# Where VectorE adds the bias to the messages, and where it makes the last block's sums, in a two-layer graph network

## The chip, the cores and the metric

The kernel runs on one core of a Trainium2 chip. The metric is the device time of one execution in microseconds (us); the kernel before takes 2246.47 us, the median of three runs (2245.61 to 2249.44). Inside a run the clock is not constant: some runs have stretches of 3.4 us at half of it (0.50).

Names used below: TensorE does matrix products and writes them into PSUM, which has eight banks here; VectorE, ScalarE and GpSimd do the elementwise work. In the profile they are PE, DVE, ACT and POOL. L386 is line 386 of the kernel.

## The reference, cut to what matters

64 graphs of 256 nodes with 256 features pass through two layers in fp32. Layer 0 has a conv branch and a message branch that meet in GRU gates; layer 1 is a graph convolution.

```python
h = relu(bn1(conv1d(xc, conv1_w, 0)))                  # xc is x with nodes and features swapped
x_conv = relu(bn2(conv1d(h, conv2_w, 8)) + xc)         # 17 taps
s = x @ w_se.T + b_se
A = exp(-dist(s)) * adj
msg = relu(x @ w_msg.T + b_msg)
x_nmp = einsum('bnm,bmd->bnd', A, msg)
gi = concat(x_conv, x_nmp) @ w_ih.T + b_ih
gh = x @ w_hh.T + b_hh                                 # r and z from gi + gh
nn_ = tanh(gi_n + r * gh_n)
x = layernorm(x + (1 - z) * nn_ + z * x)
# layer 1
h = layernorm(x)
conv = (adj @ h) @ W_rel + b_rel + h @ W_root
x = layernorm(x + x + relu(conv))
```

## The kernel before

The 64 graphs go in eight batch blocks of eight. While the gates and messages of block b run graph by graph, the conv branch of block b+1 is fed in between them: `pump()` takes the next pieces of the conv generator, butterflies of a transform on VectorE (L104, L362) and products on TensorE (L386). The order of the Python calls is the order of each engine's instructions.

The messages of graph k+3 are made while graph k passes. Two halves of the nodes go into two PSUM banks; VectorE then adds the biases, two small and two 256-wide additions. Only then are the banks free.

```python
def bank(name):
    return psum.tile([P, 512], F32, tag="ps", name=name)      # eight banks, handed out in turn

def messages(k, idle=False):
    ...
    pss = [bank("ps_msg") for _ in range(C)]
    for m, ps in enumerate(pss):
        for c in range(C):
            nc.tensor.matmul(ps[:, :D + 4], XT[k][:, c, m * P:(m + 1) * P], wms[:, c, :], ...)   # L678
    yield                                                     # <- step(msg) resumes here
    for m, ps in enumerate(pss):
        ...
        nc.vector.tensor_add(twice[:, m, :, 0:3], ...)                                           # L688
        nc.vector.tensor_add(MSG[k][:, m, :], ps[:, :D], bms[:, :D])                             # L690
    nc.scalar.activation(MSG[k], MSG[k], AF.Relu)
    ...                                                       # five small steps on GpSimd, L696 to L700

def products(b, first, sums):
    p1, p2, p3 = bank("ps_k1"), bank("ps_k2"), bank("ps_k3")  # the next three banks
    ...                                                       # 24 matmul records, L386
    def take():
        nc.scalar.copy(k1, p1)                                # L404
        ...                                                   # VectorE takes p3 and p2, L405, L406
```

The main loop, up to the last conv block, and the loop of the last batch block, which has no conv work left:

```python
for k in range(b * BG, min((b + 1) * BG, B - 1)):             # blocks 0 to 6
    ...
    msg = messages(k + 3) if k + 3 < B else None
    step(msg)                     # the eight matmuls of the messages
    step(up)                      # nn: two VectorE operations, tanh on ScalarE
    pump()                        # a piece of the next block's conv
    step(msg)                     # the four additions
    step(up)                      # w, L877, and its statistics
    pump()
    step(up)                      # h, L896
    ...

for k in range(first_k, B - 1):                               # block 7
    load(k + 3)
    load_x(k + 1)
    ga, up = block_gates(k), update(k)
    step(ga)                      # first half of the gates: seven-product form, from sums of blocks
    step(y_left)                  # output of the graph before: add, statistics (VectorE)
    step(ga)
    transposes_h(k - 1)
    step(ga)
    passing(k + 1)
    if k + 2 < B:
        factors(k + 2)
    step(ga)                      # x's part of n: eight matmuls and the addition L858
    if k + 2 < B:
        block_sums(k + 1, 0)      # four 128-wide additions each, L808 to L811
        block_sums(k + 1, 2)
    project(k - 1)
    ...
    msg = messages(k + 3) if k + 3 < B else None
    step(msg)
    step(up)
    step(msg)
    step(up)
    if k + 2 < B:
        block_sums(k + 1, 1)
    ...
```

`block_gates` takes the products of the gates (L826) out of PSUM with VectorE additions at L831.

```python
def pump():
    ...                           # conv pieces up to the share due at this point
    if STAGE.get(NB - 1) in ("inverse", "out"):
        next(sums_left, None)     # one pair of additions for the weights of the last block
    if STAGE.get(NB - 1) == "out" and (NB - 1) * BG in NMP and len(early_sums) > (done < 1e8):
        block_sums((NB - 1) * BG, early_sums.pop(0))
```

Of the kernel before, what the change touches and what calls it, by code (L numbers as in the profile page):

```python
# [17 lines left out]
B, N, D = 64, 256, 256  # L18
# [58 lines left out]
def gnn_two_layers(  # L77
# [22 lines left out]
    def bank(name):  # L100
        return psum.tile([P, 512], F32, tag="ps", name=name)
# [548 lines left out]
    def load(k):  # L650

        if k >= B:
            return
        load_xt(k)
        load_adj(k)
# [9 lines left out]
    def load_x(k):  # L665
        if k < B:
            XG[k] = work.tile([P, C, D], F32, tag="x", name="x")
            nc.sync.dma_start(out=XG[k], in_=x[k].rearrange("(c p) d -> p c d", p=P))
# [59 lines left out]
    def mask(k):  # L728
        nc.vector.tensor_mul(AT[k], AT[k], ADJ[k])
# [15 lines left out]
    def gates_rz(k, n):  # L745
        if n == 0:
            RZ[k] = (work.tile([P, C, 2 * D], F32, tag="rz", name="rz", bufs=1),
                     work.tile([P, C, 2 * D], F32, tag="gn", name="gn", bufs=1))
        q, ins = inputs(k, n)
        prz = bank("ps_rz")  # L750
        for c in range(C):
            nc.tensor.matmul(prz, XT[k][:, c, q], whh[:, c, 0:2 * D], start=(c == 0), stop=False)  # L752

        for j, i in enumerate((2, 3, 0, 1) if k == 0 else range(4)):
            nc.tensor.matmul(prz, ins[i], wih[:, i, 0:2 * D], start=False, stop=(j == 3))  # L755
        rz = RZ[k][0]

        nc.vector.tensor_add(rz[:, n, :], prz, brzn[:, :2 * D])  # L758
        nc.scalar.activation(rz[:, n, :], rz[:, n, :], AF.Tanh, scale=0.5)  # L759

    def gates_n(k, n):
        q, ins = inputs(k, n)
        pn = bank("ps_n")
        for c in range(C):
            nc.tensor.matmul(pn[:, D:], XT[k][:, c, q], whh[:, c, 2 * D:], start=(c == 0), stop=(c == C - 1))  # L765
        for i, t in enumerate(ins):
            nc.tensor.matmul(pn[:, :D], t, wih[:, i, 2 * D:], start=(i == 0), stop=(i == 3))  # L767
        nc.vector.tensor_add(RZ[k][1][:, n, :], pn, brzn[:, 2 * D:])  # L768
# [29 lines left out]
    def block_sums(k, i):  # L798

        if i == 2:  # L800
            xc, g = XC[k]
            v = xc[:, :, g, :]
        else:
            v = (XT, NMP)[i][k]
        a11, a12, a21, a22 = (v[:, c, n * P:(n + 1) * P] for n in range(C) for c in range(C))
        at = S * D + ((k % 2) * 3 + i) * 4 * P
        s1, s2, s3, s4 = (XF[:, at + j * P:at + (j + 1) * P] for j in range(4))
        nc.vector.tensor_add(s1, a21, a22)  # L808
        nc.vector.tensor_sub(s2, s1, a11)
        nc.vector.tensor_sub(s3, a11, a21)  # L810
        nc.vector.tensor_sub(s4, a12, s2)  # L811
        LEFT[k, i] = (a11, a12, s4, a22, s1, s2, s3)
# [54 lines left out]
    def update(k):  # L867

        rz, gn = RZ[k]
        nn = work.tile([P, C, D], F32, tag="nn", name="nn", bufs=1)  # L870
        stt(nn, rz[:, :, :D], 1.0, gn[:, :, D:], op0=ALU.add, op1=ALU.mult)
        stt(nn, nn, 0.5, gn[:, :, :D])
        nc.scalar.activation(nn, nn, AF.Tanh)
        yield

        w = work.tile([P, C, D], F32, tag="w", name="w", bufs=1)
        nc.vector.tensor_sub(w, XG[k], nn)  # L877
        stt(w, rz[:, :, D:], 3.0, w, op0=ALU.add, op1=ALU.mult)
        stt(w, nn, 4.0, w)
        mv = work.tile([P, C, 2], F32, tag="mv", name="mv", bufs=4)  # L880
        for n in range(C):
            stats(mv, n, w[:, n, :])


        q = work.tile([P, 2, C], F32, tag="q", name="q", bufs=4)
        nc.gpsimd.tensor_scalar(q[:, 0, :], mv[:, :, 1], 4 * EPS, None, ALU.add)
        nc.gpsimd.tensor_scalar(q[:, 1, :], mv[:, :, 1], 1 + EPS, 4 * EPS * EPS, ALU.mult, ALU.add)
        nc.gpsimd.tensor_tensor(q, q, mhalf[:, :2 * C].rearrange("p (a c) -> p a c", a=2), ALU.pow)
        sh = work.tile([P, C], F32, tag="sh", name="sh", bufs=4)
        nc.gpsimd.tensor_mul(sh, mv[:, :, 0], q[:, 0, :])  # L890
        nc.gpsimd.tensor_scalar(sh, sh, -1.0, None, ALU.mult)  # L891
        yield
        H[k] = work.tile([P, C, D], F32, tag="h", name="h", bufs=1)
        X1[k] = work.tile([P, C, D], F32, tag="x1", name="x1", bufs=2)
        for n in range(C):
            nc.vector.tensor_scalar(H[k][:, n, :], w[:, n, :], mv[:, n, 0:1], q[:, 1, n:n + 1],  # L896
                                    ALU.subtract, ALU.mult)
        for n in range(C):
            nc.scalar.activation(X1[k][:, n, :], w[:, n, :], AF.Identity, bias=sh[:, n:n + 1], scale=q[:, 0, n:n + 1])  # L899
        yield  # L900
# [14 lines left out]
    def project(k):  # L915
        hT = H[k]
        hr = work.tile([P, C, D], F32, tag="hr", name="hr", bufs=1)
        outs = []
        for n in range(C):
            ps = bank("ps_out")  # L920
            for c in range(C):
                nc.tensor.matmul(ps, hT[:, c, n * P:(n + 1) * P], wrr[:, c, :], start=(c == 0), stop=(c == C - 1))  # L922
            nc.scalar.copy(hr[:, n, :], ps[:, :D])
            outs.append(ps)
        OUTS[k] = (hr, outs)
# [29 lines left out]
    def step(g):  # L955
        if g is not None:
            next(g, None)
# [218 lines left out]
    for b in range(NB):  # L1176
        coming = conv(b + 1) if b + 1 < NB else iter(())
        done, at, goal = 0.0, 0, BG * POINTS - 6

        def pump():  # L1180
            nonlocal done, at
            at += 1
            while done < CONV_WEIGHT * at / goal:
                t = next(coming, 1e9)
                if t is None:
                    break
                done += t
            if STAGE.get(NB - 1) in ("inverse", "out"):
                next(sums_left, None)

            if STAGE.get(NB - 1) == "out" and (NB - 1) * BG in NMP and len(early_sums) > (done < 1e8):
                block_sums((NB - 1) * BG, early_sums.pop(0))

        if b == NB - 1:
            break
        for k in range(b * BG, min((b + 1) * BG, B - 1)):
            load(k + 3)
            load_x(k + 1)
            up = update(k)
            agg = None  # L1200
            gates_rz(k, 0)
            pump()
            gates_n(k, 0)
            step(y_left)
            pump()
            if k > 0:
                transposes_h(k - 1)
            pump()
            gates_rz(k, 1)
            pump()  # L1210
            if k + 1 < B:
# [4 lines that stand above are left out]
            gates_n(k, 1)  # L1216
            pump()
            if k > 0:
                project(k - 1)
            if k + 2 < B:  # L1220
                distances(k + 2)
            msg = messages(k + 3) if k + 3 < B else None
            step(msg)
            step(up)
            pump()
            step(msg)
            step(up)
            pump()
            step(up)
            pump()  # L1230
            if k + 2 < B:
                mask(k + 2)
            if k > 0:
                agg = aggregate(k - 1)
            step(agg)
            step(agg)
            pump()
            y_left = agg
        for _ in coming:
            pass  # L1240
# [5 lines left out]
    for k in range(first_k, B - 1):  # L1246
# [4 lines that stand above are left out]
        step(y_left)  # L1251
# [3 lines that stand above are left out]
        passing(k + 1)  # L1255
        if k + 2 < B:
            factors(k + 2)
        step(ga)
        if k + 2 < B:
            block_sums(k + 1, 0)  # L1260
            block_sums(k + 1, 2)
        project(k - 1)
        if k + 2 < B:
            distances(k + 2)
# [9 lines that stand above are left out]
            mask(k + 2)  # L1274
        agg = aggregate(k - 1)
        step(agg)
        step(agg)
        y_left = agg
# [44 lines left out]
```

## Time and profile before

| | kernel before |
|---|---|
| span of the profiled run | 2247.1 us |
| TensorE busy | 2205.1 us, 98% |
| VectorE busy | 1719.0 us, 76% |
| ScalarE, GpSimd busy | 773.1 us, 503.8 us |
| TensorE waits for VectorE's additions to the messages | 12.0 us, 14 times |
| TensorE waits for L831 in the last block | 7.7 us, 7 times |

Busy shares say which engine can shorten the program: only what keeps TensorE from starting counts. The prediction below shows the lines of the page, the list of waits and the order of time that this table comes from. A row of the list of waits reads: engine and line that waits, what it waits for, us in all, times, the longest. A line of the order of time reads: start, us from first start to last end, engine, line, operation, output<-input, sizes, count, and in brackets how long the engine had stood idle and what ended that.

### The profile page before, as it was taken

The page shows a single profiled execution, that of the slowest core. Times are in us where ns is not written, and L with a number is a line of the kernel's source. Part 1 is how long each engine was busy: PE and PEld are TensorE (multiplying, and loading weights), DVE is VectorE, ACT ScalarE, POOL GpSimd, SP SyncE. Part 2 cuts the span into 40 slices and gives each one's busy share as a digit, 9 for nine tenths or more (in the row PEclk, how much of TensorE's full clock was granted, in tenths as well). Part 3 has the DMA queues.
Part 4 walks back from the last instruction along what each step waited for, and adds up shares of the span by engine and source line. Part 5 has one row for each costly group of instructions (what it writes and reads, how often), then busy time and mean ns, then how long its engine had stood idle before and what let it go on. Part 6 is the DMA issues. An engine that isn't in the chain of part 4 may idle for free.

```text
span 2247.1 us, 24777 instructions
## 1 busy us (share of the span) xinstructions
PE 2205.1 (98%) x8400; PEld 1459.6 (65%) x8400; DVE 1719.0 (76%) x3322; ACT 773.1 (34%) x1594; POOL 503.8 (22%) x933
## 2 busy tenths in 40 slices
PE   8999999999999999999999999999999999999998
PEld 5776666666665676656666566666666666666665
DVE  6967988399873998649886598956989389896665
ACT  6533223532244322433224422243222532224333
POOL 0112222132122321223122231223222132122222
PEclk9999999999999999999999999999999999999999
DMA  5932442314323152233422243222432314421100
GB/s 149 318 113 66 141 135 77 103 38 151 121 76 108 54 169 83 75 103 108 139 87 76 84 131 122 76 96 69 141 116 90 99 42 137 141 71 43 43 28 20
DMA packets 212683, 226.70 MB, mean 101 GB/s; under 512 B 22103, under 2 KB 203854, under 8 KB 212558
## 3 DMA queue, kind: packets, MB, share of 16 engines
q1 hardware_dynamic: 190128, 191.27, 27.0%
q10 hardware_dynamic: 22430, 33.86, 4.3%
q8 instruction: 67, 1.10, 0.2%
q14 instruction: 58, 0.48, 0.1%
HBM read 179.22 MB, written 45.88 MB: 100 GB/s over the span
## 4 chain that ended last, share of the span: by engine, by line
PE 67%; DVE 24%; DMA 3%; issue 3%; POOL 2%; ACT 1%; SPq 0%; POOLq 0%; DVEq 0%; ACTq 0%
PE ps_k L386 14%; PE ps_rz L755 11%; DVE XF L104 9%; PE ps_rz L752 6%; PE ps_n L767 6%; PE ps_out L922 5%; PE ps_c L492 5%; PE ps_nmp L736 4%; DMA w<-w2m 3%; PE ps_msg L678 3%; PE ps_n L765 3%; PE ps_out L934 3%; DVE XF L362 2%; DVE XF L456 2%; DVE nn L104 1%
## 5 line engine op out<-in xcount | busy, mean ns | idle before, releaser
L104 DVE SCALAR_TENSOR_TENSOR XF<-XF 128x512 f32<-128x512 f32 (+2 forms) x800 | 508.0, 666 | 7.4
L386 PE MATMUL ps_k<-w,XF 128*128 128x256 f32 x1316 | 297.8, 381 | 17.6 <-DVE st L688 12.0
L386 PEld LDWEIGHTS ps_k<-w,XF 128*128 128x128 f32 x1316 | 246.7, 190 | 63.3 <-issue 24.9
L696 POOL TENSOR_TENSOR sq<-st 128x6 f32<-128x6 f32 x64 | 13.8, 215 | 1219.2 <-DVE st L688 1169.3
L922 PE MATMUL ps_out<-wrr,hT 128*128 128x512 f32 x504 | 226.7, 592 | 0.0
L759 ACT ACTIVATE rz<-rz 128x512 f32<-128x512 f32 x114 | 71.8, 630 | 446.4 <-DVE rz L758 446.4
L752 PE MATMUL ps_rz<-whh,xT 128*128 128x512 f32 x456 | 214.4, 592 | 0.0
L755 PE MATMUL ps_rz<-wih,nmp 128*128 128x512 f32 x456 | 214.3, 592 | 0.0
L755 PE MATMUL ps_rz<-wih,xc 128*128 128x512 f32 x456 | 214.3, 592 | 0.0
L768 DVE TENSOR_TENSOR gn<-ps_n,brzn 128x512 f32<-128x512 f32 x114 | 78.3, 687 | 171.2 <-PE ps_n L767 171.2
L899 ACT ACTIVATE x<-w,sh,q 128x256 f32<-128x256 f32 x126 | 68.8, 593 | 342.7 <-POOL sh L891 342.7
L755 PEld LDWEIGHTS ps_rz<-wih,xc 128*128 128x128 f32 x456 | 86.6, 190 | 109.1 <-issue 109.1
L755 PEld LDWEIGHTS ps_rz<-wih,nmp 128*128 128x128 f32 x456 | 86.6, 190 | 109.1 <-issue 109.1
L758 DVE TENSOR_TENSOR rz<-ps_rz,brzn 128x512 f32<-128x512 f32 x114 | 77.7, 682 | 104.3 <-PE ps_rz L755 104.3
L922 PEld LDWEIGHTS ps_out<-wrr,hT 128*128 128x128 f32 x504 | 95.2, 190 | 93.6 <-issue 81.8
L678 PE MATMUL ps_msg<-wms,xT 128*128 128x260 f32 x512 | 129.9, 396 | 0.0
L362 DVE TENSOR_TENSOR XF<-XF 128x512 f32<-128x512 f32 (+3 forms) x128 | 125.4, 1004 | 1.7
L736 PE MATMUL ps_nmp<-AT,msg 128*128 128x256 f32 x512 | 121.0, 379 | 0.0
L752 PEld LDWEIGHTS ps_rz<-whh,xT 128*128 128x128 f32 x456 | 82.1, 190 | 57.8 <-issue 55.0
L934 PE MATMUL ps_out<-hr,adj 128*128 128x256 f32 x504 | 119.5, 380 | 0.0
L492 PE MATMUL ps_c<-xTc,w 128*128 128x512 f32 x256 | 116.2, 596 | 2.3 <-ACT xTc L482 2.3
L765 PE MATMUL ps_n<-whh,xT 128*128 128x256 f32 x456 | 117.2, 379 | 0.0
(200 smaller groups left out, 3738.1 us busy)
## 6 DMA issues: line engine op xcount, KB each, us to landing
w<-w2m SPq DMA_DIRECT2D x105, 768.0 KB, 5.8
xn<-in_x_dram SPq DMA_DIRECT2D x32, 512.0 KB, 4.2
xt<-xTc ACTq DMA_DIRECT2D x32, 512.0 KB, 3.2
xT<-xt SPq DMA_DIRECT2D x64, 256.0 KB, 3.0
xb<-in_x_dram SPq DMA_DIRECT2D x32, 512.0 KB, 5.1
adj<-in_adjT_dram SPq DMA_DIRECT2D x64, 256.0 KB, 2.7
x<-in_x_dram SPq DMA_DIRECT2D x64, 256.0 KB, 3.0
out_dram<-y ACTq DMA_DIRECT2D x63, 256.0 KB, 2.3
```

Of the source, the lines that this page charges most:

```text
L104: nc.vector.scalar_tensor_tensor(o, in0, s, in1, op0=op0, op1=op1)
L362: (nc.vector.tensor_add if add else nc.vector.tensor_sub)(sl(o, n), sl(a, n), sl(b, n))
L386: nc.tensor.matmul(ps, X[:, slot, c * P:(c + 1) * P], w(m, c), start=first and c == 0, stop=(c == C - 1), skip_group_check=True)
L492: nc.tensor.matmul(pss[o], w1[:, c, o * P:(o + 1) * P], xTc[:, c, :], start=(c == 0), stop=(c == C - 1))
L678: nc.tensor.matmul(ps[:, :D + 4], XT[k][:, c, m * P:(m + 1) * P], wms[:, c, :], start=(c == 0), stop=(c == C - 1 and not idle))
L736: nc.tensor.matmul(ps[:, d * N:(d + 1) * N], MSG[k][:, m, d * P:(d + 1) * P], AT[k][:, m, :], start=(m == 0), stop=(m == C - 1))
L752: nc.tensor.matmul(prz, XT[k][:, c, q], whh[:, c, 0:2 * D], start=(c == 0), stop=False)
L755: nc.tensor.matmul(prz, ins[i], wih[:, i, 0:2 * D], start=False, stop=(j == 3))
L765: nc.tensor.matmul(pn[:, D:], XT[k][:, c, q], whh[:, c, 2 * D:], start=(c == 0), stop=(c == C - 1))
L767: nc.tensor.matmul(pn[:, :D], t, wih[:, i, 2 * D:], start=(i == 0), stop=(i == 3))
L922: nc.tensor.matmul(ps, hT[:, c, n * P:(n + 1) * P], wrr[:, c, :], start=(c == 0), stop=(c == C - 1))
L934: nc.tensor.matmul(po, ADJ[k][:, m, n * P:(n + 1) * P], hr[:, m, :], start=False, stop=(m == C - 1), skip_group_check=True)
```

## The change

The first part puts VectorE's four additions to the messages ahead of the conv piece, so that the two banks come free sooner. The second part, in the last block, puts eight additions of sums ahead of the addition that takes x's part of n out of PSUM, into time in which VectorE waits for that product. No instruction is added or removed.

```diff
             step(msg)
             step(up)
+            step(msg)
             pump()
-            step(msg)
             step(up)
@@ the last block
         if k + 2 < B:
             factors(k + 2)
-        step(ga)
-        if k + 2 < B:
             block_sums(k + 1, 0)
             block_sums(k + 1, 2)
+        step(ga)
         project(k - 1)
```

## The prediction

> **What bounds the kernel now.** I read the page's busy shares first, then the list of TensorE's waits, then the order of time around them. TensorE sets the time: matmuls fill 2205.1 of 2247.1 us at a clock of 0.998, VectorE is busy 76%. So the change can only win what TensorE stands still.
>
> ```profile
> span 2247.1 us, 24777 instructions
> PE 2205.1 (98%) x8400; PEld 1459.6 (65%) x8400; DVE 1719.0 (76%) x3322; ACT 773.1 (34%) x1594; POOL 503.8 (22%) x933
> ```
>
> The list of waits, TensorE's alone, splits the 42 us of standstill (columns: total us, times, longest):
>
> ```profile
> PE ps_k L386 <- DVE st L688: 12.0, 14, 0.9
> PE ps_a L826 <- DVE XF L831: 7.7, 7, 1.8
> PE ps_k L386 <- DMA w<-w2m: 4.7, 12, 1.1
> PE ps_c L492 <- ACT xTc L482: 2.3, 3, 0.8
> ```
>
> Row one is the part that the change aims at: conv products (L386) wait until VectorE has added the bias to the messages (L688, L690). It is 14 times, so twice in each of seven batch blocks of eight graphs. Row two lies in the last batch block. The order of time shows the first kind (start, us, engine, line, and in brackets idle before):
>
> ```profile
> 546.77 2.02 PE L678 MATMUL ps_msg<-wms,xT 128*128 128x260 f32 x8
> 547.87 2.16 DVE L362 TENSOR_TENSOR XF<-XF 128x1024 f32<-128x1024 f32 x3
> 548.63 1.03 PE L386 MATMUL ps_k<-w,XF 128*128 128x256 f32 x4
> 549.94 0.16 DVE L688 TENSOR_TENSOR st<-ps_msg,bms 128x6 f32<-128x6 f32 x1
> 550.01 0.42 DVE L690 TENSOR_TENSOR msg<-ps_msg,bms 128x256 f32<-128x256 f32 x1
> 550.58 4.55 PE L386 MATMUL ps_k<-w,XF 128*128 128x256 f32 x20 [0.92 <-DVE st L688]
> ...
> 589.87 2.61 DVE L104 SCALAR_TENSOR_TENSOR XF<-XF 128x512 f32<-128x512 f32 x4
> 591.22 1.03 PE L386 MATMUL ps_k<-w,XF 128*128 128x256 f32 x4
> 592.39 0.16 DVE L688 TENSOR_TENSOR st<-ps_msg,bms 128x6 f32<-128x6 f32 x1
> 593.03 4.55 PE L386 MATMUL ps_k<-w,XF 128*128 128x256 f32 x20 [0.79 <-DVE st L688]
> ```
>
> After four records of a product TensorE stops: the product's second bank is the one that the first half of the messages still occupies. VectorE had those messages since 547.95, but did three butterflies of the conv branch first. I call these graphs the seventh and eighth of a block, as the pattern repeats every 270 us.
>
> **What the Trainium skill says.** (1) "PSUM — Partial Sum Buffer", section "Engine vs sequencer instructions": the queues of VectorE, ScalarE and GpSimd are strictly first in, first out, and matmuls start in program order. The trace agrees: messages ready at 547.95 were added at 549.94, behind the butterflies. (2) "Perfetto Trace Analysis", section "Optimization Strategy": a gap that repeats on the saturated engine can mean that the next tile finds no room. Agrees: 0.92 and 0.79 us recur in every block. (3) "GPSIMD Engine Reference", section "1. Specifications": GpSimd shares SBUF interfaces with VectorE, with contention when a VectorE instruction has two SBUF inputs. Agrees: one small multiply took 2.25 us beside the 2048-wide additions at 521, and 0.2 us elsewhere. The new order puts conv additions beside GpSimd's five steps on the messages; a rival below.
>
> **Part one, by steps.** Nothing is added or removed; in the built program TensorE's order is the same, and on VectorE the four additions (2 x 0.16 and 2 x 0.42 us, overlapping to 0.80) go ahead of the conv piece. On ScalarE the messages' relu goes ahead of four conv relus once a block, where VectorE idles anyway.
> What is lost now, counted to the end of 24 records. An unbroken run took 5.34 us (534.63 to 539.97). The seventh graph's took 550.58 + 4.55 - 548.63 = 6.50, the eighth's 593.03 + 4.55 - 591.22 = 6.36. So 1.16 and 1.02 us are lost (more than the gaps, as draining and refilling the array shows as busy). 2.18 x 7 = 15.3 us.
> Is the bank free in time afterwards? Where VectorE waits for messages, it begins 1.18 us after their first matmul (2060.61 to 2061.79 in the last block), the second half begins at 2.06, and the next operation at 2.47. The first bank is thus free at 1.18 + 0.08 + 0.42 = 1.68. TensorE wants it 1.86 us (546.77 to 548.63) plus four records of 0.216 later, at 2.72: about 1.0 us to spare; the second bank similarly 0.9. Both waits go entirely.
> What it costs VectorE. It now waits for the messages where it did conv work. Its next operation (w, L877) begins, from the first message matmul, at 2.47 plus the conv piece: seventh graph 2.47 + 2.07 (547.87 to 549.94) = 4.54 instead of 3.97 (+0.57), eighth 2.47 + 2.52 (589.87 to 592.39) = 4.99 instead of 3.84 (+1.15), first of the next block +1.2, second +1.1. In the fourth to sixth the messages come before VectorE is free, or there is no conv piece: no change.
> Does TensorE feel that? VectorE's idle before it next waits for TensorE must cover both shifts. Seventh graph: 1.16 + 0.57 = 1.73 against 1.89 idle at 575.68: covered. Eighth: 1.02 + 1.15 = 2.17. The nearest need is a bank at 611.79 whose copy by ScalarE ended at 609.60 behind VectorE's addition: 2.19 to spare, so 0.02 remains. In the two graphs after, the smallest margins are 2.38 (h at 637.07) against 1.2, and 1.57 (a ScalarE relu at 664.76) against 1.1. All hold, one barely.
> One place does not hold: the last conv block also carries additions of weight blocks, TensorE already waits 1.30 us at 2005.36 for ScalarE behind VectorE, and h at 1990.25 has 0.30 to spare. Of the 2.17 us only 1.17 (idle at 1970.33) is covered, so 1.0 us comes back as longer waits. Part one: -15.3 + 1.0 = -14.3 us.
>
> **Part two, the last batch block.** In six graphs eight additions (8 x 0.29, overlapped 1.86 us) move from behind the addition to x's part of n (L858) to ahead of it.
>
> ```profile
> 2052.98 0.56 DVE L831 TENSOR_TENSOR XF<-ps_c,XF 128x384 f32<-128x384 f32 x1 [0.70 <-PE ps_c L826]
> 2056.65 0.69 DVE L858 TENSOR_TENSOR XF<-ps_n,brzn 128x512 f32<-128x512 f32 x1 [3.12 <-PE ps_n L856]
> 2059.84 0.69 DVE L104 SCALAR_TENSOR_TENSOR nn<-nn,XF 128x512 f32<-128x512 f32 x1
> 2060.61 2.02 PE L678 MATMUL ps_msg<-wms,xT 128*128 128x260 f32 x8
> 2061.44 0.63 ACT L873 ACTIVATE nn<-nn 128x512 f32<-128x512 f32 x1
> 2061.79 0.16 DVE L688 TENSOR_TENSOR st<-ps_msg,bms 128x6 f32<-128x6 f32 x1 [1.25 <-PE ps_msg L678]
> ```
>
> They fit into the 3.12 us of idle (2053.54 + 1.86 = 2055.40, before 2056.65), and nn ends 1.86 us earlier. But then VectorE waits for the messages again, until the same 2061.79: its wait grows from 1.25 to 3.11 us. ScalarE's tanh comes no earlier either, as the exponentials stand ahead of it. All that leads to L831, for which TensorE waits 7.7 us, begins at L688, after that wait. So idle time moves and TensorE gains 0.
>
> **The rivals.** A: VectorE's lateness reaches TensorE in full. 0.57 + 1.15 + 1.2 + 1.1 = 4.02 us a block, 28.1 in seven, less 15.3: 2259 us. For it: VectorE is over 90% busy in these graphs. Against: the margins listed. If only the thinnest gives way, by 0.5 us a block, 3.5 of the gain go: 2235.5.
> B: the products then wait for their weights instead. The DMA's row has 4.7 us, and the product at 564.64 starts as they land. If they came no earlier, all 15.3 us would be taken back: 2246. Against: they are issued at 557.82, right behind the adjacency block's issue at 556.89, which waits for the aggregation matmuls that end at 556.86; these move with TensorE, so the weights do too.
> C: part two also frees L831 earlier and its seven waits (7.7 us) vanish: 2224. Against: the 1.25 us of idle ahead of L688.
> D: GpSimd is slowed beside the conv piece and returns h late. Its five steps end 2.5 us after the additions; even 2.3 us more leaves them done before q is asked for (3.4 us after w begins, and w is later by the conv piece). Worth 0 to 1 us.
>
> **Range and chances.** 2246.5 - 14.3 = 2232.2; I say 2232. The three runs of before spread over 3.8 us. Downwards the most is 15.3 plus such noise: 2229. Upwards the thin margins (3.5 us) and some waits for DMA: 2239. The 2% bounds are at 2202 and 2291; no rival comes near: faster 0.01, within 0.98, slower 0.01.
>
> **What would show it.** In the changed profile the row of L386 waiting on L688 should be gone or under 1 us; runs of 24 product records should be unbroken; the 7.7 us for L831 should stand; VectorE's idle ahead of L858 should shrink from 21.6 us in all by some 11, and that ahead of L688 grow. TensorE's wait near the end of the last conv block should be longer by up to 1.0 us. I am wrong if waits for a bank appear after the eighth graph's product, if the DMA row grows beyond 10 us, or if L831's waits shrink.

## The result, and the profile after

The changed kernel takes 2235.61 us (median of four runs, 2234.21 to 2235.93); the kernel before, in the same rounds, 2247.95 (2245.61 to 2251.47). Ratios here are the mean time of one kernel's fast runs over the mean of the other's in the same rounds, so not quite the ratio of these medians: 0.9943, with a 95% interval of 0.9925 to 0.9960. That is within 2% of the kernel before; the point prediction was 2232 and the range 2229 to 2239.

The page of the kernel after, its first lines:

```profile
span 2233.9 us, 24739 instructions
...
PE 2201.5 (99%) x8400; PEld 1460.0 (65%) x8400; DVE 1720.5 (77%) x3322; ACT 773.3 (35%) x1594; POOL 531.9 (24%) x933
```

TensorE does the same 8400 instructions in 13.2 us less span. Of this 9.6 us is standstill (42.0 before, 2233.9 - 2201.5 = 32.4 after): the 12.0 us of L688, less 2.4 us by which other waits grew. The rest, 3.6 us, is busy time. A product that stops shows more of it than one that runs through (5.58 us against 5.34), and 14 stops make 3.3 us of that.

TensorE's waits in the kernel after:

```profile
PE ps_a L826 <- DVE XF L831: 8.6, 7, 1.8
PE ps_k L386 <- DMA w<-w2m: 4.5, 9, 0.9
PE ps_c L492 <- ACT xTc L482: 3.0, 3, 1.5
```

The row that the change aimed at, 12.0 us for L688, is gone altogether. The row of the DMA did not take it over (4.7 before). The row of L831 grew, by 0.9 us: that is not in the prediction.

The same stretch as in the prediction, in the order of time of the kernel after; first the block's seventh graph, then its eighth:

```profile
544.35 2.02 PE L678 MATMUL ps_msg<-wms,xT 128*128 128x260 f32 x8
545.53 0.17 DVE L688 TENSOR_TENSOR st<-ps_msg,bms 128x6 f32<-128x6 f32 x1
...
546.20 5.34 PE L386 MATMUL ps_k<-w,XF 128*128 128x256 f32 x24
546.82 2.15 DVE L362 TENSOR_TENSOR XF<-XF 128x1024 f32<-128x1024 f32 x3
548.89 0.68 DVE L877 TENSOR_TENSOR w<-x,nn 128x512 f32<-128x512 f32 x1
...
586.23 2.02 PE L678 MATMUL ps_msg<-wms,xT 128*128 128x260 f32 x8
...
588.09 5.34 PE L386 MATMUL ps_k<-w,XF 128*128 128x256 f32 x24
588.70 2.61 DVE L104 SCALAR_TENSOR_TENSOR XF<-XF 128x512 f32<-128x512 f32 x4
591.23 0.68 DVE L877 TENSOR_TENSOR w<-x,nn 128x512 f32<-128x512 f32 x1
```

The additions start 1.18 us after the first matmul of the messages, the butterflies come behind them, and 24 product records run in 5.34 us without a stop, against 6.50 and 6.36 before. The price is visible too: `w` begins 4.54 us (548.89 - 544.35) and 5.00 us (591.23 - 586.23) after that first matmul, against 3.97 and 3.84 before.

In the last block the list of VectorE's waits for x's part of n went from 21.6 us to 10.4 (kernel after):

```profile
DVE XF L858 <- PE ps_n L856: 10.4, 7, 2.9
```

and the wait ahead of the messages' first addition, 1.25 us in the prediction's lines, became 2.92 (order of time of the kernel after):

```profile
2048.63 0.16 DVE L688 TENSOR_TENSOR st<-ps_msg,bms 128x6 f32<-128x6 f32 x1 [2.92 <-PE ps_msg L678]
```

So the second part did what it set out to do on VectorE, and the freed time turned into a longer wait one step further on.

**Where the time came from.** I took the interval from one graph's first message matmul to the next graph's, in both orders of time, and added the differences (after minus before) over the seven blocks by the graph's place in its block:

| stretch | predicted | measured |
|---|---|---|
| product of the seventh graph, 7 times | 7 x -1.16 = -8.1 | -7.2 |
| product of the eighth graph, 7 times | 7 x -1.02 = -7.1 | -7.9 |
| behind it in the last conv block | +1.0 | +0.87 |
| last graph ahead of the last block | 0 | +0.93 |
| start of the program | 0 | -1.1 |
| everything else | 0 | +1.2 |
| sum | -14.3 | -13.2 |

The last two rows above the sum are not of the change. All eleven kernels below leave the start alone and have it 0.5 to 1.2 us shorter too: the profiled run of the kernel before has one of the stretches at half the clock there, from 7.5 to 10.9 us. "Everything else" lies in the graphs just ahead of the seventh, and part two alone, which does nothing in the seven blocks, has +1.2 there as well. The first two rows carry the scatter of single executions. Over more of them it shrinks: the mean of the seven profiled runs with the new order in both graphs (without the five additions and the last experiment), less the mean of the three with the old one (the kernel before, part two alone, the other six graphs), is -7.9 and -7.1 us. The fourth row is real.

**The row that the prediction lacks.** In the last graph ahead of the last block, `pump()` holds no conv work but four of the last block's sums. The order of time of the kernel before:

```profile
2035.19 0.28 DVE L811 TENSOR_TENSOR XF<-xc,XF 128x128 f32<-128x128 f32 x1
2036.73 0.17 DVE L688 TENSOR_TENSOR st<-ps_msg,bms 128x6 f32<-128x6 f32 x1 [1.26 <-PE ps_msg L678]
2038.02 0.68 DVE L877 TENSOR_TENSOR w<-x,nn 128x512 f32<-128x512 f32 x1
...
2047.51 1.99 PE L826 MATMUL ps_a<-wsum,XF 128*128 128x256 f32 x6 [0.89 <-DVE XF L831]
```

and of the kernel after:

```profile
2022.65 0.17 DVE L688 TENSOR_TENSOR st<-ps_msg,bms 128x6 f32<-128x6 f32 x1 [2.19 <-PE ps_msg L678]
2023.94 0.28 DVE L808 TENSOR_TENSOR XF<-xc 128x128 f32<-128x128 f32 x1
2024.87 0.69 DVE L877 TENSOR_TENSOR w<-x,nn 128x512 f32<-128x512 f32 x1
...
2034.35 1.99 PE L826 MATMUL ps_a<-wsum,XF 128*128 128x256 f32 x6 [1.81 <-DVE XF L831]
```

Before, the sums ended while VectorE would have waited for the messages anyway. After, VectorE waits 2.19 us with nothing to do, and the sums come between the additions and `w`. That chain is what TensorE waits for at L831: 0.89 became 1.81 us.

### The profile page after: what moved, and what is told of

Its sections match the earlier page's. It is cut to its first block, busy times and chain, and to the rows that moved or that the text cites. A ratio compares the mean times of both kernels' runs of the same rounds, so it can differ in the third digit from the quotient of the medians.

```text
span 2233.9 us, 24739 instructions
## 1 busy us (share of the span) xinstructions
PE 2201.5 (99%) x8400; PEld 1460.0 (65%) x8400; DVE 1720.5 (77%) x3322; ACT 773.3 (35%) x1594; POOL 531.9 (24%) x933
## 4 chain that ended last, share of the span: by engine, by line
PE 73%; DVE 19%; DMA 3%; issue 2%; POOL 2%; ACT 1%; SPq 0%; POOLq 0%; DVEq 0%; ACTq 0%
PE ps_k L386 13%; PE ps_rz L755 12%; PE ps_out L922 8%; DVE XF L104 6%; PE ps_rz L752 6%; PE ps_n L767 6%; PE ps_c L492 5%; PE ps_msg L678 4%; PE ps_nmp L736 4%; PE ps_n L765 3%; DMA w<-w2m 2%; PE ps_out L934 2%; PE ps_w L230 2%; DVE XF L456 2%; DVE bst L864 2%
## 5 line engine op out<-in xcount | busy, mean ns | idle before, releaser
L104 DVE SCALAR_TENSOR_TENSOR XF<-XF 128x512 f32<-128x512 f32 (+2 forms) x800 | 507.9, 666 | 7.4
L934 PE MATMUL ps_out<-hr,adj 128*128 128x256 f32 x504 | 119.5, 380 | 0.0
```

Source lines behind the costliest of these rows:

```text
L104: nc.vector.scalar_tensor_tensor(o, in0, s, in1, op0=op0, op1=op1)
L934: nc.tensor.matmul(po, ADJ[k][:, m, n * P:(n + 1) * P], hr[:, m, :], start=False, stop=(m == C - 1), skip_group_check=True)
```

## The experiments

All eleven kernels gave correct results. The theory: part one wins what the two stops of the product cost, in the seventh and eighth graph alone; part two wins nothing, as the wait for the messages stands behind it; and the missing 0.9 us is the graph with the block sums. The rivals: A, that VectorE's lateness comes back to TensorE; C, that part two has a share of the gain; and that the earlier additions in the other six graphs help or harm. Runs of one batch used one chip and share the runs of the kernel before.

### First batch: the parts, and the graphs (five rounds)

The change again, unaltered:

> The changed kernel once more, as the measure for the other runs of this chip. 2235 us, ratio 0.994. Both theories: the same as in the first measurement. From the profile: TensorE's waits for L688 stay gone; the 1.1 us by which the start of the program (to the first messages after it) was shorter in the first profile should differ again, as it is not of the change; the rest of the gain, 12 us, should stay.

2235.11 us (2233.66 to 2236.41), kernel before 2247.24 (2246.13 to 2250.19), ratio 0.9947 (0.9934 to 0.9959). The gain repeats on another chip.

Part one alone, taken from the kernel before:

```diff
             step(up)
-            pump()
             step(msg)
+            pump()
             step(up)
```

> Only the messages' additions ahead of the conv piece, the sums of the last block where they were. My theory (part two moves idle time alone): the same as the whole change within 0.5 us, ratio 0.994. Rival (part two is worth some of its 1.86 us in six graphs, up to 11 us): 2240 to 2246 us.

2238.32 us (2235.64 to 2240.47), ratio 0.9959 (0.9947 to 0.9972). Its profiled run had the span 2233.9 us, the same as the whole change, and 8.6 us of waits for L831.

Part two alone, taken from the kernel before:

```diff
+            block_sums(k + 1, 0)
+            block_sums(k + 1, 2)
         step(ga)
-        if k + 2 < B:
-            block_sums(k + 1, 0)
-            block_sums(k + 1, 2)
```

> Only the sums of the last block ahead of x's part of n. My theory: as before within 0.5 us beyond noise, ratio 1.000; TensorE's seven waits for L831 keep 7 to 8 us, and VectorE's idle ahead of L858 shrinks by 11 us while that ahead of L688 grows by it. Rival (the sums delayed the chain to L831): 2238 to 2242 us.

2248.34 us (2247.05 to 2249.75), ratio 1.0005 (0.9993 to 1.0018). The waits stood where they were: 11.9 us for L688, 7.7 for L831. The first part is the gain and rival C falls. The timing alone would leave part two some 0.1% on top of part one: part one alone lies 3.2 us above the whole change, where I expected 0.5 at most. But the two intervals overlap, and the orders of time settle it. From the last messages ahead of the last block to the end, the profiled runs take 211.5 us in the kernel before and with part two alone, and 212.5 and 212.4 us with part one alone and with both. Part two moves nothing there, and it does nothing elsewhere; the rest of the 3.2 us stays unexplained scatter.

The additions go ahead only in the two graphs whose product stopped (k mod 8 is 3 or 4, as the messages are three graphs ahead), with part two kept:

```diff
             step(up)
-            step(msg)
+            if k % BG in (3, 4):
+                step(msg)
             pump()
+            step(msg)
             step(up)
```

> The additions go ahead in only two of eight graphs, those with a product right behind the messages (k mod 8 of 3 and 4), with part two. My theory: the whole gain is from these, so at least the gain of the whole change; and the graph ahead of the last block (k = 55) gets back 0.9 us of TensorE's first wait for L831 (1.8 to 0.9 us), so about 1 us under the changed kernel, 2234 to 2235 us. Rival (moving them helps VectorE's flow in all graphs): part of the gain is lost, 2238 or more.

2233.71 us (2232.47 to 2234.51), ratio 0.9939 (0.9925 to 0.9952). All of the gain is in these two graphs. In its order of time the four block sums end ahead of the messages' additions again, and the list of TensorE's waits has L831 back at its old size:

```profile
PE ps_a L826 <- DVE XF L831: 7.7, 7, 1.8
```

The difference in time to the whole change, 1.4 us between the medians, is of the right sign and size but inside the intervals; the 0.9 us is shown by the wait, not by the clock.

### Second batch: the counterpart, half, and too much (three rounds)

The complement of the run above: the additions go ahead in the other six graphs, part two kept.

```diff
-            step(msg)
+            if k % BG not in (3, 4):
+                step(msg)
             pump()
+            step(msg)
```

> The opposite: the additions go ahead in the six other graphs of a block, not in k mod 8 of 3 and 4. My theory: nothing of the gain, TensorE's 14 waits for L688 keep 12 us; and 0.9 us is lost ahead of the last block: ratio 1.000, within 2 us of before. Rival (VectorE's flow): part of the gain, 2238 to 2244.

2248.55 us (2247.98 to 2250.95), kernel before 2248.88 (2246.77 to 2254.94), ratio 0.9998 (0.9982 to 1.0014). The wait for L688 stands at 11.9 us, L831 has the 8.6. In the six graphs the new order brings nothing, and the 0.9 us of cost belongs to them.

Only the first half's additions go ahead in the two graphs; the second half's stay behind the conv piece. The rest is the kernel before.

```diff
             nc.vector.tensor_add(MSG[k][:, m, :], ps[:, :D], bms[:, :D])
+            if halves and m == 0:
+                yield
@@ the main loop
-            msg = messages(k + 3) if k + 3 < B else None
+            msg = messages(k + 3, halves=k % BG in (3, 4)) if k + 3 < B else None
             step(msg)
             step(up)
+            if k % BG in (3, 4):
+                step(msg)
             pump()
             step(msg)
```

> The kernel before, but in the two graphs only the FIRST half of the messages is added ahead of the conv piece, the second half behind it. My theory (the product's second bank is the first half's and its third bank the second half's): TensorE runs eight records of the product instead of four and then waits for the second half: by hand 0.74 us in the one graph (third bank wanted at 3.58, free at 4.32 us) and 1.2 us in the other (free at 4.77), 13 to 14 us in all where it was 12: no gain, 2247 to 2250 us. Rival (half the additions ahead gives half the gain): 2240.

2246.84 us (2245.46 to 2252.26), ratio 0.9993 (0.9973 to 1.0012): no gain that can be told from none. Its order of time, in the seventh graph:

```profile
549.01 1.89 PE L386 MATMUL ps_k<-w,XF 128*128 128x256 f32 x8
551.45 3.69 PE L386 MATMUL ps_k<-w,XF 128*128 128x256 f32 x16 [0.55 <-DVE msg L690]
```

The product now gets through eight records instead of four and stops at its third bank, which the second half of the messages holds. The waits add up to 10.9 us instead of 12.0. So it is the banks, one after the other, that stop the product, and freeing one of the two moves the stop by four records. I had put the gaps at 0.74 and 1.2 us; they measured 0.55 and 1.01. The profiled run of this kernel also had 9.0 us of waits for weights from a DMA; in the timed mean nothing of that is left to see, which shows how far a single execution strays.

The kernel after, with five additions that nobody needs ahead of the messages' additions in the two graphs:

```diff
             step(up)
+            if k % BG in (3, 4):
+                for _ in range(5):
+                    nc.vector.tensor_add(scratch, brzn[:, :D], brzn[:, D:2 * D])
             step(msg)
             pump()
```

> The changed kernel with five useless additions of 256 columns (about 1.7 us on VectorE) ahead of the messages' additions in the two graphs. My theory: the additions had 1.0 us to spare, so 0.7 us a block (k mod 8 of 3) plus 0.15 us (k mod 8 of 4) come back as waits for L688, 6 us in seven blocks, and up to 0.5 us a block more through VectorE's lateness later: 2241 to 2246 us. Rival (the gain is only from the order of the work on VectorE and not from a bank freed in time): VectorE has over 300 us of idle and hides it, 2236.

2252.80 us (2250.45 to 2255.01), ratio 1.0018 (0.9999 to 1.0037). Its order of time:

```profile
548.13 2.26 DVE L1228 TENSOR_TENSOR scratch<-brzn 128x256 f32<-128x256 f32 x5
548.90 1.03 PE L386 MATMUL ps_k<-w,XF 128*128 128x256 f32 x4
550.95 4.55 PE L386 MATMUL ps_k<-w,XF 128*128 128x256 f32 x20 [1.02 <-DVE st L688]
```

The direction was as expected, the size was not: I had put it at 2241 to 2246 us. The five additions took 2.26 us instead of the 1.7 that I had reckoned, so the stops were 1.02 us (here) and 0.43 (eighth graph) instead of 0.7 and 0.15. Its list of waits, the first row and the one that is new:

```profile
PE ps_k L386 <- DVE st L688: 10.1, 14, 1.0
...
PE ps_rz L752 <- ACT XF L404: 1.8, 5, 0.4
```

10.1 us of stops, 14 times 0.24 us by which a stop lengthens the busy time (6.50 - 5.34 - 0.92, an estimate from the prediction's lines) and 1.8 us make 15.3 us; against the changed kernel's ratio the timed loss is 0.0071 to 0.0075, some 16 to 17 us. The new row is the bank that the prediction found to have 0.02 us to spare. In the kernel after that margin held, and here, with VectorE later still, it gave way. So rival A was no phantom: the change stops just short of it.

The kernel after, with the last block's sums behind the messages' additions instead of ahead of x's part of n:

```diff
             factors(k + 2)
-            block_sums(k + 1, 0)
-            block_sums(k + 1, 2)
         step(ga)
@@ further down
         step(msg)
+        if k + 2 < B:
+            block_sums(k + 1, 0)
+            block_sums(k + 1, 2)
         step(up)
```

> The changed kernel with the last block's sums (1.86 us in six graphs) BEHIND the messages' additions, so after VectorE's wait for them. My theory (the chain to L831 begins at L688; only ahead of it is idle time free): each of these six TensorE waits for L831 grows by 1.5 to 1.9 us: 9 to 11 us more than the changed kernel, 2245 to 2247. Rival (the place of the sums does not matter at all, as VectorE is only two thirds busy there): 2235 to 2236.

2246.69 us (2242.66 to 2247.46), ratio 0.9984 (0.9966 to 1.0002), so 0.0037 to 0.0041, or 8 to 9 us, worse than the change. Its waits grew by 8.0 us (15.2 + 1.4 - 8.6):

```profile
PE ps_a L826 <- DVE XF L831: 15.2, 7, 2.3
PE ps_b L826 <- DVE XF L808: 1.4, 5, 0.3
```

The order of time shows more than these waits: the last block, counted from its first messages, took 199.0 us against 186.5 in the kernel after, so 12.5 us more. Five of the stops for L831 are 2.3 us long, and behind two of these the granted clock fell to 0.50 for 3.4 us: six records that take 1.99 us elsewhere took 2.92 behind the first of them, and these two graphs lost 1.6 to 1.7 us more than the other stopped ones. Why two of five is not shown.

Work that VectorE does behind the wait for the messages is paid at L831; work ahead of that wait is free. Both places that part two chooses between lie ahead of it.

### Third batch: is it better still? (five rounds)

If that is right, whatever can leave the stretch between the messages and L831 is won. The output of the graph before (L104 and four operations of statistics, 1.8 us in the kernel after, from 2057.14 to 2058.95) stands there. This kernel is the change with that work behind the first four L831:

```diff
         step(ga)
-        step(y_left)
         step(ga)
+        step(y_left)
+        step(y_left)
         transposes_h(k - 1)
@@ the end of the loop
         step(agg)
-        step(agg)
         y_left = agg
+    step(y_left)
     last_graph(y_left, B - 1)
```

> The changed kernel, and in the last batch block the output's residual addition and statistics (stt and four statistics, 1.8 us on VectorE) go from ahead of the first four additions of the gates (L831) to behind them. My theory (TensorE's wait there is for L831 at the end of VectorE's row that begins at the messages): those additions come 1.8 us earlier, the wait of 1.0 us in five graphs and of 1.8 in two goes, 8.6 us in the list and 1 to 2 us more of refilling: 8 to 10 us under the changed kernel, 2225 to 2228 us. Rival (the output's statistics then hold up the transposed h by ScalarE or the next additions): the wait comes back at ps_b or ps_out, 2235.

2226.57 us (2225.48 to 2229.35), kernel before 2246.70 (2243.76 to 2252.12), ratio 0.9911 (0.9899 to 0.9924). In its list of waits six of the seven for L831 are gone; the one left is the block's first graph, whose output work the main loop had already put ahead:

```profile
PE ps_a L826 <- DVE XF L831: 1.8, 1, 1.8
```

This edit and the additions in two graphs only, together:

```diff
-            step(msg)
+            if k % BG in (3, 4):
+                step(msg)
             pump()
+            step(msg)
@@ the last block: the edit of the run above
```

> Both: the additions ahead in two of eight graphs only, and the later statistics of the output. The two gains lie in different stretches, so they should add: 2224 to 2227 us, ratio 0.990.

2225.34 us (2224.64 to 2225.78, four runs), ratio 0.9904 (0.9891 to 0.9918). The remaining wait for L831 is 0.9 us, once.

Both, and in the eighth graph one conv butterfly stays ahead of the additions, in time that VectorE waits for the messages anyway:

```diff
+            if k % BG == 4:
+                t = next(coming)
+                done += t or 0.0
             if k % BG in (3, 4):
                 step(msg)
```

> As the last one, but in the graph k mod 8 of 4 one conv butterfly (0.6 us) stays ahead of the messages' additions, where VectorE would wait 0.59 us for the messages. My theory: VectorE's later work of that graph is 0.6 us less late; TensorE feels it only in the last conv block (its loss of 0.7 to 0.9 us there shrinks by 0.6): 0 to 1 us under the last one, within noise in time; in the profile w of that graph begins 4.4 instead of 5.0 us after the first message matmul. No wait for L688 comes back. Rival: the butterfly makes the bank late, and 7 x 0.3 us come back.

2223.37 us (2222.53 to 2226.62), ratio 0.9902 (0.9888 to 0.9916). The product stays unbroken, `w` begins 4.40 us after the messages' first matmul instead of 5.00, and no stop for a bank comes back. The time cannot be told from that of the run above. These three kernels beat both the kernel before (by 0.9 to 1.0%) and the change (by 0.3 to 0.5%).

## Why the prediction was right, and the term it missed

- **The bound and the bank.** Right: the row of waits for L688 was 12.0 us and is gone. Two graphs a block carry all of it, and both halves must go ahead: with one, 10.9 us of waits stayed.
- **What a stop costs.** Right: -15.3 us was the term, and the two rows measured -7.2 and -7.9, together -15.1. One pair of runs misses the split of -8.1 and -7.1; the means over ten profiled runs, -7.9 and -7.1, meet it.
- **What VectorE pays.** Right in size: `w` begins at 4.54 and 5.00 us after the messages' first matmul, where 4.54 and 4.99 stood. The margins held, the 0.02 us one too; the five additions show that it was real. In the last conv block +0.87 us came back, where +1.0 stood, but not as the longer wait that was forecast: the 1.30 us ahead of L724 stayed at 1.29, and 0.67 us came at h (L909), which had 0.30 us to spare and now waits 0.33. Two readings were off without harm: the second bank has 1.0 us to spare, not 0.9, and VectorE is over 90% busy behind the eighth graph's messages (95% from 589.4 to 626) but 84% busy from the seventh's to the eighth's.
- **The step that failed.** "In the fourth to sixth the messages come before VectorE is free, or there is no conv piece: no change." With the seventh, eighth, first and second that covers seven of the eight places in a block; the third is passed over. In the blocks that repeat, nothing happens there: `w` begins 2.47 us after the first message matmul in both kernels. But the last graph ahead of the last block has this place, and there `pump()`, without a conv piece, makes four block sums that lay hidden in VectorE's wait for the messages, so `w` went from 2.47 to 3.40 us. The missing term is +0.93 us; it stands in L831's wait (0.89 to 1.81), and undoing part one outside the two graphs took it out again. For the same reason the sentence that the 7.7 us for L831 should stand was wrong by that much. With it the sum is -13.4 us; the two sets of timed runs gave -12.8 (0.9943) and -11.9 (0.9947), and the last 0.6 to 1.5 us lie within both intervals and stay unexplained.
- **Part two.** Right: nothing alone, L858's wait from 21.6 to 10.4 us (11 less were predicted), and the wait ahead of L688 grew in its place. Moving the sums behind that wait cost 8 to 9 us (12.5 in the order of time), which shows the wait as the wall that the argument took it for.
- **The rivals.** A (2259 us) and C (2224 us) fell by the first batch. B (weights from the DMA) fell with 4.5 us against 4.7. D was half right: GpSimd did slow down, by 28.1 us of busy time in all (503.8 to 531.9); the longest of its L697 steps took 2.22 us instead of 1.17. What may have come of it are three new waits for h, which needs GpSimd's result, of 0.7 us in all; whether GpSimd or VectorE made h late there was not tried.

The Trainium skill, "TensorE: Matmul & The Clock Gate", section "Step-by-step: what each phase is for", has the drain of one matmul overlap the fill of the next in an unbroken stream. The traces agree in kind: the product broken once is busy 1.03 + 4.55 = 5.58 us, unbroken 5.34, so a stop costs 0.24 us beyond the gap that the list of waits shows. The ends of matmuls are modelled in these profiles, so how the loss divides into gap and busy time is the profile's; the loss itself comes out of starts alone: from the product's first record to the matmul behind it (L934) are 6.34 us before (548.63 to 554.97) and 5.18 after (546.20 to 551.38), 1.16 us less.

## What to carry to other kernels

When a pool of PSUM banks goes round, work that empties banks should stand ahead of work that nobody waits for; count the stop by the length of the whole run of matmuls, not by the gap alone. Before moving work behind a wait, list everything that sits in that place in every iteration, the odd last one too, as what was hidden in the wait becomes time on the path. Work moved from one side to the other of an operation is free only as far as the next wait on the same queue; the gain lies in taking work out of the stretch between the last wait and what the bounding engine needs.

## What the Trainium skill lacked or had wrong

- "TensorE: Matmul & The Clock Gate", "Step-by-step: what each phase is for", gives the overlap of drain and fill, and the section on single matmul latency has only bf16; no cost of a stop in the middle of an fp32 product was found: here 0.24 us beyond a gap of 0.92 us, and 0.23 beyond one of 0.79.
- "GPSIMD Engine Reference", "1. Specifications", names the contention with VectorE instructions of two SBUF inputs without a size, and the rule of who blocks whom in "SBUF — State Buffer", "Who interferes with whom", has no time for such a pair either: the same small GpSimd addition (L697) took 0.62 us with the old order and 1.16 us beside the butterflies in the seventh graph, 0.62 again beside those in the eighth, and up to 2.22 us in the kernel after.
- "Vector Engine (DVE) Microarchitecture Reference", "5.2 Measured stream behaviour on trn2", has a pace for back-to-back instructions, but none was found for short additions that write one tile over again: five of 256 columns took 2.26 us, 0.46 us from start to start ((2.26 - 0.42) / 4, with 0.42 for one such addition at L690), where butterflies of 256 columns in the kernel before also come 0.34 us apart (L305 at 572.24, L303 at 572.58). Whether the shared output is the cause was not tried.
